# Cross-attention, 16 batches: context of 192 as 128 + 64, loads in order of use, mask on GpSimd

## Chip, core and metric

One core of one Trainium2 chip. The time is that of one execution in microseconds of device time; the median of three runs is given, and one more execution was profiled. Engines: PE (TensorE), DVE (VectorE), ACT (ScalarE), POOL (GpSimd), and SP, whose queue issues most of the DMAs here.

## The reference, cut to what matters

All tensors are float32. B = 16 batches, S = 256 queries of width 256, 77 context rows of width 192, H = 8 heads of D = 256. The mask (16 x 77) is all ones in the inputs.

```python
Q = (img_embed @ Wq).reshape(B, -1, H, D).transpose(0, 2, 1, 3)
K = (sent_embed @ Wk).reshape(B, -1, H, D).transpose(0, 2, 1, 3)
V = (sent_embed @ Wv).reshape(B, -1, H, D).transpose(0, 2, 1, 3)
score = jnp.einsum('bhqd,bhkd->bhqk', Q, K) / math.sqrt(D)
score = jnp.where(mask, score, -jnp.inf)
attn = jax.nn.softmax(score, axis=-1)
ctx = jnp.einsum('bhqk,bhkd->bqhd', attn, V).reshape(B, -1, H * D)
out = ctx @ Wo + img_embed
mu = jnp.mean(out, axis=-1, keepdims=True)
var = jnp.var(out, axis=-1, keepdims=True)
return (out - mu) * jax.lax.rsqrt(var + EPS) * gamma + beta
```

## The kernel before

The weights are folded per head, so that neither Q, K nor V is ever formed. In the setup, `gT` holds Wk Wq^T of each head (tile `pg`, L156) and `u` holds Wv Wo (tile `pu`, L191). For both, slices of the weights are transposed on PE (`transposed`, L135) and copied out of PSUM by `evacuate` (L103), which alternates between ACT and DVE. The context is transposed to `cT` (tile `pc`, L170), and GpSimd copies it into `cM` (the first 64 rows of each batch) and `cR` (the other 13).

The width 192 of the context lies on 96 partitions twice, so every product over it is two matmuls of 96 rows that add up in one PSUM bank. There are three such products: `pr` (L206, rows 64 to 76 of the values, for all batches), `pa` (L264, keys times `gT`: for a group of four batches, 16 outputs of 308 columns), and `pv` (L282, values for a pair of batches, four outputs of 512 columns).

The results of `pr` go through `stage` and a DRAM tensor `scratch` to `vr`, in another layout: eight DMAs per `stage` and one back, all issued by SP. `stage` lies in the memory of the setup pool `wload`; when that pool closes, the pool of `a` takes the memory over, so that the first copies into `a` wait until the DMAs have read `stage`.

The main loop runs over 32 tiles of 128 queries, 8 per group of four batches. `prepare_group` transposes x (tile `px`, copied to `xT`) and makes `a`; `prepare_pair`, every fourth tile, makes `vw` from `pv` with sixteen copies, eight on ACT and eight on DVE. `scores_and_softmax` computes the scores (tile `ps`, two banks; 4 matmuls) and on DVE adds the mask's bias (`s`, L312, which frees `ps`), takes the maximum and subtracts it; ACT takes the exponential (`e`), DVE the sum (`den`, `rden`), GpSimd the product `p`. `attend`, two tiles later, transposes `p` (`pp`, `pq`), copies it to `pT` on ACT, and multiplies with `vw` and `vr` (`po`); DVE adds x. `normalise_group` does the layer norm's last step for eight tiles at once and sends four DMAs.

Each engine runs its instructions in a fixed order. A scheduler that knows the tiles and their buffers sets that order at build time, so an instruction can stand at another place than in the code. PSUM has eight banks: two score buffers of two banks, two for transposes (`ps_tr`), two for products (`ps_mm`).

The mask's arithmetic is on DVE: `bias` is 0 or -3e38, `live` is 1 for a batch with a key left and not a number for one without.

Of the kernel before, what the change touches and what calls it, by code (L numbers as in the profile page):

```python
# [21 lines left out]
MASKED = 3.0e38  # L22

# [10 lines left out]
def kernel(  # L34
# [16 lines left out]
    LP = DL // 2  # L51
    CR = 112
# [10 lines left out]
    assert NCR * CR == B * S2 and NG * GB == B and DI == 2 * P and D == 2 * P  # L63
# [25 lines left out]
    xg_of = {}  # L89
# [6 lines left out]
    dram = ctx.enter_context(tc.tile_pool(name="dram", bufs=1, space=bass.MemoryType.DRAM))  # L96
    scratch = dram.tile([B, H, KR, DI], F32, tag="scratch", name="scratch")

    cM = const.tile([LP, 2, B, KM], F32, tag="cM", name="cM")
    cR = const.tile([LP, 2, B, KR], F32, tag="cR", name="cR")  # L100
    evacs = [0]

    def evacuate(dst, src):  # L103
        evacs[0] += 1
        if evacs[0] % 2:
            nc.scalar.copy(dst, src)  # L106
        else:
            nc.vector.tensor_copy(dst, src)  # L108


    with tc.tile_pool(name="wload", bufs=1) as wp, tc.tile_pool(name="wt", bufs=2) as wt:
# [21 lines left out]
        load_x(1)  # L133
# [16 lines left out]
        for h in range(H):  # L150
# [3 lines left out]
            for lc in range(2):  # L154
                for dc in range(2):
                    nc.tensor.matmul(  # L156
                        pg[:LP, lc, :],
                        wkT[:, dc, lc * LP : (lc + 1) * LP],
# [4 lines left out]
            nc.scalar.mul(gT[:, :, h, :], pg[:LP], D ** -0.5)  # L163

        for r in range(0, NCR, 2):
            n = min(2, NCR - r)
            pc = ps_tr.tile([P, 4, P], F32, tag="tr", name=f"pc_{r}")
            for lc in range(2):
                for j in range(n):
                    nc.tensor.transpose(  # L170
                        pc[:LP, 2 * lc + j, :CR],
                        c_sb[:, r + j, lc * LP : (lc + 1) * LP],
                        ident[:CR, :CR],
                    )
# [208 lines left out]
    for t in range(NT + AHEAD):  # L383
# [44 lines left out]
```

## Time and profile before

| | us |
|---|---|
| median of 3 runs (lowest, highest) | 415.19 (415.14, 417.15) |
| the profiled execution | 414.41 |
| its span (first to last instruction) | 412.4 |
| PE busy | 352.2 (85% of the span) |
| DVE busy | 228.2 (55%) |
| ACT busy | 115.0 (28%) |
| POOL busy | 50.3 (12%) |

The share is a mean over stages. The setup ends at 124 us with the first `ps`; then four groups of about 74 us follow, each opened by its `px` and `pa` (those of the first group stand in the setup). In a row of the timeline, the number in brackets is the time that the engine stood idle just before, with what ended it. A matmul of float32 shows as two records; the duration of a record is its whole way through the array, and the next one starts before it ends, so the distance between starts is what a record costs in a stream.

### The profile page before, as it was taken

Reading aid. Unit: us, or ns where it says so; the run is one execution under the profiler, and the core shown is the slowest. Engines: PE = TensorE matmul, PEld = TensorE weight load, DVE = VectorE, ACT = ScalarE, POOL = GpSimd, SP = SyncE. Lnnn points to the kernel's source line nnn. Section 1 sums busy time; section 2 is a strip of 40 time slices with the busy share of each in tenths; the row PEclk is TensorE's granted clock in tenths of the full one; section 3 lists DMA queues with packets and bytes.
Section 4 is the critical chain, followed back from the end, with each engine's and each line's share of the span. In section 5 each row is a group of like instructions: output and inputs, shape, how many; then the busy total and the mean of one; then the engine's idle time right before and its main releaser. Section 6 shows DMA issues by size and latency. Waiting matters only on the chain.

```text
span 412.4 us, 4082 instructions
## 1 busy us (share of the span) xinstructions
PE 352.2 (85%) x1462; PEld 245.6 (60%) x1462; DVE 228.2 (55%) x492; ACT 115.0 (28%) x246; POOL 50.3 (12%) x74
## 2 busy tenths in 40 slices
PE   0604989994799999999999999999999999999972
PEld 0503767633474657767576676758757775775851
DVE  0004132222025996942699886258988725798884
ACT  1200342111123242231443322243333223334231
POOL 0000002000001121310111221011121201032120
PEclk9955999998599999999999999999999999999997
DMA  8999000026500000000006000000500000030002
GB/s 219 262 287 325 3 0 0 2 63 150 119 2 0 0 0 2 0 2 0 0 2 203 0 2 2 0 0 2 175 28 2 0 2 0 0 103 2 0 1 102
DMA packets 17005, 21.22 MB, mean 51 GB/s; under 512 B 714, under 2 KB 15770, under 8 KB 16794
## 3 DMA queue, kind: packets, MB, share of 16 engines
q1 hardware_dynamic: 13258, 16.36, 14.1%
q10 hardware_dynamic: 3728, 4.62, 4.0%
q8 instruction: 11, 0.18, 0.2%
q14 instruction: 8, 0.07, 0.0%
HBM read 15.08 MB, written 5.90 MB: 51 GB/s over the span
## 4 chain that ended last, share of the span: by engine, by line
PE 47%; DVE 32%; DMA 9%; ACT 7%; issue 3%; SPq 1%; ACTq 0%; DVEq 0%
PE pa L264 16%; PE pv L282 9%; DMA m_i<-in_mask_BxS_if_dram 5%; DVE s L320 5%; DVE top L319 4%; DVE s L312 4%; PE po L354 4%; ACT e L324 4%; PE pg L156 4%; DVE xg L370 4%; PE pu L191 4%; PE ps L304 3%; DVE den L326 3%; PE pr L206 3%; DVE xg L373 3%
## 5 line engine op out<-in xcount | busy, mean ns | idle before, releaser
L333 POOL TENSOR_TENSOR p<-e,rden 128x512 f32<-128x512 f32 x64 | 47.0, 755 | 289.6 <-DVE rden L329 156.3
L264 PE MATMUL pa<-cT,gT 96*128 96x308 f32 x256 | 71.8, 438 | 8.6 <-ACT a L106 8.6
L304 PE MATMUL ps<-a,xT 128*128 128x308 f32 x256 | 75.4, 422 | 0.0
L264 PEld LDWEIGHTS pa<-cT,gT 96*128 96x128 f32 x256 | 49.6, 198 | 26.5 <-ACT a L106 9.0
L354 PE MATMUL po<-vw,pT 128*128 128x256 f32 x256 | 61.1, 381 | 4.7 <-ACT pT L348 4.7
L282 PE MATMUL pv<-u,cM 96*128 96x512 f32 x128 | 60.0, 602 | 3.9 <-ACT vw L292 2.7
L354 PEld LDWEIGHTS po<-vw,pT 128*128 128x128 f32 x256 | 48.1, 190 | 17.2 <-ACT pT L348 7.6
L304 PEld LDWEIGHTS ps<-a,xT 128*128 128x128 f32 x256 | 46.5, 190 | 13.4 <-issue 1.4
L108 DVE COPY a<-pa 128x308 f32<-128x308 f32 x32 | 15.3, 479 | 58.3 <-PE pa L264 49.3
L282 PEld LDWEIGHTS pv<-u,cM 96*128 96x128 f32 x128 | 23.0, 189 | 31.4 <-issue 19.8
L324 ACT ACTIVATE e<-s 128x616 f32<-128x616 f32 x32 | 22.9, 716 | 55.6 <-DVE s L320 55.6
L292 DVE COPY vw<-pv 64x256 f32<-64x256 f32 x64 | 26.9, 421 | 15.1 <-PE pv L282 14.1
L156 PE MATMUL pg<-wqT,wkT 128*96 128x256 f32 x64 | 19.0, 449 | 19.0 <-DVE wkT L108 19.0
L348 ACT COPY pT<-pp 128x512 f32<-128x512 f32 x32 | 18.6, 583 | 56.4 <-PE pp L347 56.2
L326 DVE TENSOR_REDUCE den<-e 128x8 f32<-128x616 f32 x32 | 25.3, 791 | 14.8 <-ACT e L324 14.6
L292 ACT COPY vw<-pv 64x256 f32<-64x256 f32 x64 | 23.4, 365 | 29.4 <-PE pv L282 28.5
L106 ACT COPY a<-pa 128x308 f32<-128x308 f32 x32 | 13.3, 417 | 60.4 <-PE pa L264 50.9
L312 DVE TENSOR_TENSOR s<-ps,bias 128x616 f32<-128x616 f32 x32 | 25.0, 782 | 6.4 <-PE ps L304 6.4
L156 PEld LDWEIGHTS pg<-wqT,wkT 128*96 128x96 f32 x64 | 11.6, 192 | 24.3 <-DVE wkT L108 20.6
L320 DVE TENSOR_TENSOR s<-s,top 128x616 f32<-128x616 f32 x32 | 25.7, 803 | 0.7
L319 DVE TENSOR_REDUCE top<-s 128x8 f32<-128x616 f32 x32 | 25.1, 783 | 0.3
L347 PEld LDWEIGHTS pp<-ident,p 128*128 128x128 f32 x128 | 16.0, 141 | 10.5 <-issue 5.3
(57 smaller groups left out, 305.6 us busy)
## 6 DMA issues: line engine op xcount, KB each, us to landing
xg<-in_x_dram SPq DMA_DIRECT2D x4, 1024.0 KB
out_dram<-xg SPq DMA_DIRECT2D x16, 256.0 KB
wq_sb<-in_L_xattn_Wq_dram SPq DMA_DIRECT2D x2, 1024.0 KB
wo_sb<-in_L_xattn_Wo_dram ACTq DMA_DIRECT2D x1, 2048.0 KB
scratch<-stage SPq DMA_DIRECT2D x16, 104.0 KB
vr<-scratch SPq DMA_DIRECT2D x2, 832.0 KB
wk_sb<-in_L_xattn_Wk_dram ACTq DMA_DIRECT2D x2, 768.0 KB
wv_sb<-in_L_xattn_Wv_dram SPq DMA_DIRECT2D x1, 1536.0 KB
```

The source lines that it names most:

```text
L156: nc.tensor.matmul(pg[:LP, lc, :], wkT[:, dc, lc * LP : (lc + 1) * LP], wqT[:, dc, :], start=(dc == 0), stop=(dc == 1),)
L264: nc.tensor.matmul(pa.rearrange("p b k -> p (b k)"), gT[:, lc, h, dc * P : (dc + 1) * P], cT[:, lc, g * GB * S2 : (g + 1) * GB * S2], star ...
L282: nc.tensor.matmul(pv.rearrange("p h d -> p (h d)"), cM[:, lc, b : b + 2, :].rearrange("p b k -> p (b k)"), u[:, lc, 2 * n : 2 * n + 2, :] ...
L292: copy(vw[i][half * KM : (half + 1) * KM, n, :], pv[i * KM : (i + 1) * KM, half, :],)
L304: nc.tensor.matmul(ps[:, hh, :HK], xT_of[g][:, dc, j * P : (j + 1) * P], a_of[g][:, dc, bl, hh * 4 : hh * 4 + 4, :].rearrange("p h k -> p ...
L312: nc.vector.tensor_tensor(s.rearrange("p (a h) k -> p a h k", a=2), ps[:, :, :HK].rearrange("p a (h k) -> p a h k", k=S2), bias[:, b, :].u ...
L319: nc.vector.tensor_reduce(top, s, AX.X, ALU.max)
L320: nc.vector.tensor_tensor(s, s, top.unsqueeze(2).to_broadcast([P, H, S2]), ALU.subtract)
L324: nc.scalar.activation(e, s, AF.Exp)
L326: nc.vector.tensor_reduce(den, e, AX.X, ALU.add)
L333: nc.gpsimd.tensor_tensor(part, e[:, :, keys], rden.unsqueeze(2).to_broadcast(list(part.shape)), ALU.mult,)
L354: nc.tensor.matmul(po, pT[:, n, :], vw_of[b][:, n, :], start=(n == 0), stop=False)
```

## The change

- The context is split as 128 + 64. The first part (`cA`, `gA`, `uA`) fills all rows of PE. The second (`cB`, `gB`, `uB`) has 64 rows; `cB` is held twice, on partitions 0 to 63 and 64 to 127, and `gB` and `uB` hold even parts in the lower half and odd ones in the upper.
- A helper `products` issues four matmuls of 128 rows, then four of 64 rows that alternate between the halves, each into its own bank; all copies follow after the eight. It is used for `pr`, `pa` and `pv` (not shown: it reads as `pr` with `cMA` and `cMB`, and its 16 copies follow product by product). In the built program the 64-row matmuls carry a tile size of 64 x 128 and a tile position of row 0 or 64; all others have 128 x 128.
- `ps_mm` has four banks, `ps_sc` one score buffer instead of two.
- Loads: context first (half by ACT, half by SP), then x of group 0, then `wq` and `wk` in slices of two heads, `wv` and `wo` in halves, then x of group 1, the mask, gamma and beta, nearly all by SP.
- The context and x of group 0 are transposed before the weights. `pg` and `pu` are copied out by two instructions each (the 128-row and the 64-row part); of `pg`, ACT copies the first and DVE the second.
- The mask's arithmetic is on GpSimd, as products over halves of the keys.
- The last group is normalised in two parts: six tiles after tile 29, the other two at the end.

```diff
-    ps_sc = ctx.enter_context(tc.tile_pool(name="ps_sc", bufs=2, space=PSUM))
+    ps_sc = ctx.enter_context(tc.tile_pool(name="ps_sc", bufs=1, space=PSUM))
...
-    ps_mm = ctx.enter_context(tc.tile_pool(name="ps_mm", bufs=2, space=PSUM))
+    ps_mm = ctx.enter_context(tc.tile_pool(name="ps_mm", bufs=4, space=PSUM))
...
+    gA = const.tile([P, H, DI], F32, tag="gA", name="gA")
+    gB = const.tile([P, NF, DI], F32, tag="gB", name="gB")
+    uA = const.tile([P, H, DI], F32, tag="uA", name="uA")
+    uB = const.tile([P, NF // 2, 2, DI], F32, tag="uB", name="uB")
...
+    def half(i):
+        return slice(i * LB, (i + 1) * LB)
...
+    def products(outs, weightA, weightB, movingA, movingB):
+        for i in range(4):
+            nc.tensor.matmul(outs[i], weightA(i), movingA(i), start=True, stop=False)
+        for i in range(4):
+            nc.tensor.matmul(outs[i], weightB(i), movingB(i), start=False, stop=True)
...
-        half = H * D // 2
-        for i in range(2):
-            cols = slice(i * half, (i + 1) * half)
+        wo_r = wo.rearrange("(t p) f -> p t f", p=P)
+        mid = NCR // 2
+        nc.scalar.dma_start(c_sb[:, :mid, :], c_rows[:, :mid, :])
+        nc.sync.dma_start(c_sb[:, mid:, :], c_rows[:, mid:, :])
+        load_x(0)
+        for h in range(0, H, 2):
+            cols = slice(h * D, (h + 2) * D)
             nc.sync.dma_start(wq_sb[:, :, cols], wq_r[:, :, cols])
-            nc.scalar.dma_start(wk_sb[:, :, cols], wk_r[:, :, cols])
-        nc.scalar.dma_start(c_sb, c_rows)
-        nc.sync.dma_start(wv_sb, wv_r)
-        nc.scalar.dma_start(wo_sb, wo.rearrange("(t p) f -> p t f", p=P))
-        load_x(0)
+            nc.sync.dma_start(wk_sb[:, :, cols], wk_r[:, :, cols])
+        for h in range(0, H, 4):
+            cols = slice(h * D, (h + 4) * D)
+            nc.sync.dma_start(wv_sb[:, :, cols], wv_r[:, :, cols])
+            nc.sync.dma_start(wo_sb[:, 2 * h : 2 * h + 8, :], wo_r[:, 2 * h : 2 * h + 8, :])
+        load_x(1)
         nc.sync.dma_start(m_i, mask.rearrange("b k -> (b k)").partition_broadcast(P))
         nc.sync.dma_start(gam, gamma.partition_broadcast(P))
         nc.sync.dma_start(bet, beta.partition_broadcast(P))
-        load_x(1)
...
+            rows = slice(r * CR, (r + n) * CR)
+            evacuate(flat(cA)[:, rows].rearrange("p (j m) -> p j m", m=CR), pc[:, :n, :CR])
+            for i in range(2):
+                evacuate(
+                    flat(cB)[half(i), rows].rearrange("p (j m) -> p j m", m=CR),
+                    pc[LB:, 2 : 2 + n, :CR],
+                )
...
+        transpose_x(0)
...
+            nc.scalar.mul(gA[:, h, :], pg[:, 0, :], D ** -0.5)
+            nc.vector.tensor_scalar(
+                gB[half(h % 2), h // 2, :], pg[LB:, 1, :], D ** -0.5, None, ALU.mult
+            )
...
-            evacuate(u[:, :, h, :], pu[:LP])
+            evacuate(uA[:, h, :], pu[:, 0, :])
+            n = h // 2
+            evacuate(uB[half(n % 2), n // 2, h % 2, :], pu[LB:, 1, :])
+        nc.gpsimd.tensor_scalar(bias_f, m_i, 0.0, None, ALU.is_equal)
+        none = wp.tile([P, B, S2 // 2], F32, tag="none", name="none")
+        left, n = bias, S2
+        while n > 1:
+            n, odd = n // 2, n % 2
+            nc.gpsimd.tensor_tensor(none[:, :, :n], left[:, :, :n], left[:, :, n : 2 * n], ALU.mult)
+            if odd:
+                nc.gpsimd.tensor_tensor(
+                    none[:, :, :1], none[:, :, :1], left[:, :, 2 * n : 2 * n + 1], ALU.mult
+                )
+            left = none
+        none = none[:, :, 0]
+        nc.gpsimd.tensor_scalar(none, none, MASKED, MASKED, ALU.mult, ALU.mult)
+        nc.gpsimd.tensor_tensor(live, none, none, ALU.subtract)
+        nc.gpsimd.tensor_scalar(live, live, 1.0, None, ALU.add)
+        nc.gpsimd.tensor_scalar(bias_f, bias_f, -MASKED, None, ALU.mult)
...
+            products(
+                pr,
+                lambda n: flat(cRA[:, batches, :]),
+                lambda n: flat(cRB[half(n % 2), batches, :]),
+                lambda n: flat(uA[:, 2 * n : 2 * n + 2, :]),
+                lambda n: flat(uB[half(n % 2), n // 2, :, :]),
+            )
+            for n in range(NF):
+                evacuate(flat(stage[:, 2 * n : 2 * n + 2, :]), pr[n])
...
+            pa = [
+                ps_mm.tile([P, GB, S2], F32, tag="mm", name=f"pa_{g}_{n}_{i}") for i in range(4)
+            ]
+            products(
+                [flat(o) for o in pa],
+                lambda i: gA[:, 2 * n + i % 2, i // 2 * P : (i // 2 + 1) * P],
+                lambda i: gB[half(i % 2), n, i // 2 * P : (i // 2 + 1) * P],
+                lambda i: flat(cA[:, batches, :]),
+                lambda i: flat(cB[half(i % 2), batches, :]),
+            )
+            for i in range(4):
+                evacuate(a[:, i // 2, :, 2 * n + i % 2, :], pa[i])
...
-            if d % GT == GT - 1:
-                normalise_group(d // GT)
-                if d // GT + 2 < NG:
-                    load_x(d // GT + 2)
+            if d // GT == NG - 1:
+                if d % GT == GT - QT - 1:
+                    normalise(d // GT, 0, GT - QT)
+                elif d % GT == GT - 1:
+                    normalise(d // GT, GT - QT, GT)
+            elif d % GT == GT - 1:
+                normalise(d // GT, 0, GT)
+            if d % GT == GT - 1 and d // GT + 2 < NG:
+                load_x(d // GT + 2)
```

On DVE near the start of the program, before: `wkT` is the transposed key weight of a head, `m_i` the mask as loaded, `some` and `live` results of the mask.

```order
L108 COPY wkT_0_123<-p_wkT_0_124 128x384
L230 TENSOR_SCALAR bias_80<-m_i_101 128x1232
L232 TENSOR_REDUCE some_477<-bias_80 128x16
L233 RECIPROCAL live_81<-some_477 128x16
L235 TENSOR_SCALAR bias_80<-bias_80 128x1232
L108 COPY wkT_1_143<-p_wkT_1_144 128x384
L234 TENSOR_TENSOR live_81<-live_81,some_477 128x16
```

And after, the same place, behind the copies of the context and x:

```order
L127 COPY xT_0_178<-px_0_6_197 128x2x256
L127 COPY wkT_0_210<-p_wkT_0_211 128x384
L235 TENSOR_SCALAR gB_80<-pg_0_217 64x256
L127 COPY wkT_1_231<-p_wkT_1_232 128x384
L235 TENSOR_SCALAR gB_80<-pg_1_238 64x256
L127 COPY wkT_2_252<-p_wkT_2_253 128x384
```

The mask has left DVE's queue; between two `wkT` copies there stands now the copy of the 64-row part of `pg` of the head before.

On PE after the first `ps` of a group (tile 16, the third group), before: the products `pv` of a pair are mixed with the work of the tiles 14, 15 and 17.

```order
L282 MATMUL pv_8_2_1548<-u_78,cM_88 128x512 x2
L347 MATMUL pp_14_1563<-ident_70,p_14_1358 128x128 x2
L350 MATMUL pq_14_1569<-ident_70,p_14_1358 104x128
L304 MATMUL ps_17_1582<-a_2_1446,xT_2_1421 128x308
L282 MATMUL pv_8_3_1555<-u_78,cM_88 128x512 x2
L354 MATMUL po_14_1572<-vw_7_1252,pT_14_1562 128x256 x4
L355 MATMUL po_14_1572<-vr_82,pT_14_1562 128x256
L304 MATMUL ps_17_1582<-a_2_1446,xT_2_1421 128x308 x3
L347 MATMUL pp_15_1603<-ident_70,p_15_1398 128x128 x4
L350 MATMUL pq_15_1609<-ident_70,p_15_1398 104x128
L304 MATMUL ps_18_1648<-a_2_1446,xT_2_1421 128x308 x2
L354 MATMUL po_15_1612<-vw_7_1252,pT_15_1602 128x256 x4
```

After:

```order
L151 MATMUL pv_8_3_1580<-uB_82,cMB_86 128x512
L396 MATMUL pp_14_1606<-ident_72,p_14_1401 128x128 x4
L399 MATMUL pq_14_1612<-ident_72,p_14_1401 104x128
L353 MATMUL ps_17_1625<-a_2_1489,xT_2_1464 128x308 x2
L403 MATMUL po_14_1615<-vw_7_1295,pT_14_1605 128x256 x4
L404 MATMUL po_14_1615<-vr_89,pT_14_1605 128x256
L353 MATMUL ps_17_1625<-a_2_1489,xT_2_1464 128x308 x2
L396 MATMUL pp_15_1646<-ident_72,p_15_1441 128x128 x4
L399 MATMUL pq_15_1652<-ident_72,p_15_1441 104x128
L353 MATMUL ps_18_1691<-a_2_1489,xT_2_1464 128x308
L403 MATMUL po_15_1655<-vw_7_1295,pT_15_1645 128x256 x4
```

The eight matmuls of `pv` now stand in one piece ahead of the transposes `pp_14`; `po` stands between pieces of `ps`, as it did.

## Rows read from the trace of the kernel before

**Rows 1.** Page part 2: PE's busy tenths in 40 slices of 10.3 us

```profile
PE   0604989994799999999999999999999999999972
```

**Rows 2.** Windows: stretch, each engine's busy us (count), granted PE clock, DMA share, GB/s

```profile
0.00:20.00 20.00, 6.82 (x28) 5.24 (x28) 0.62 (x2) 3.63 (x5) 0.70 (x6) 1.00 0.94 241
20.00:40.00 20.00, 3.72 (x10) 2.52 (x11) 3.69 (x6) 0.00 (x0) 0.00 (x0) 0.52 1.06 312
...
106.00:112.00 6.00, 5.89 (x12) 3.91 (x13) 0.68 (x2) 0.47 (x2) 0.00 (x0) 0.50 0.69 145
```

**Rows 3.** Timeline 0 to 50 us: start, us, engine, line, operation [idle before, releaser]

```profile
32.55 0.80 DVE L230 TENSOR_SCALAR bias<-m_i 128x1232 f32<-128x1232 int32 x1 [19.34 <-DMA m_i<-in_mask_BxS_if_dram]
...
36.28 3.73 PE L156 MATMUL pg<-wqT,wkT 128*96 128x256 f32 x8 [17.91 <-DVE wkT L108]
...
44.25 1.97 PE L156 MATMUL pg<-wqT,wkT 128*96 128x256 f32 x8 [0.21 <-DVE wkT L108]
...
47.20 1.97 PE L156 MATMUL pg<-wqT,wkT 128*96 128x256 f32 x8 [0.21 <-DVE wkT L108]
```

**Rows 4.** Timeline 62 to 128 us, setup's second half

```profile
62.30 3.69 PE L191 MATMUL pu<-wo_sb,wvT 128*96 128x256 f32 x16
...
79.78 13.90 PE L206 MATMUL pr<-u,cR 96*104 96x512 f32 x32
...
87.62 7.15 SPq L218 DMA_DIRECT2D scratch<-stage  x9
...
105.63 0.42 ACT L106 COPY a<-pa 128x308 f32<-128x308 f32 x1 [9.49 <-DMA scratch<-stage]
...
124.04 2.24 PE L304 MATMUL ps<-a,xT 128*128 128x308 f32 x8
```

**Rows 5.** Groups by form: line, engine, tiles, shapes, count, busy, mean ns, idle before

```profile
L304 PE MATMUL ps<-a,xT 128*128 128x308 f32 x256 | 75.4, 422 | 0.0
...
L292 DVE COPY vw<-pv 64x256 f32<-64x256 f32 x64 | 26.9, 421 | 15.1 <-PE pv L282 14.1
...
L292 ACT COPY vw<-pv 64x256 f32<-64x256 f32 x64 | 23.4, 365 | 29.4 <-PE pv L282 28.5
...
L206 PE MATMUL pr<-u,cR 96*104 96x512 f32 x32 | 13.9, 592 | 0.0
...
L333 POOL TENSOR_TENSOR p<-e,rden 128x104 f32<-128x104 f32 x32 | 14.4, 451 | 0.0
...
L108 DVE COPY cT<-pc 96x224 f32<-96x224 f32 x5 | 1.8, 385 | 3.3 <-ACT cT L106 3.3
```

**Rows 6.** Timeline 251 to 342 us, one group of eight tiles

```profile
251.69 15.71 PE L264 MATMUL pa<-cT,gT 96*128 96x308 f32 x60
...
267.25 2.24 PE L304 MATMUL ps<-a,xT 128*128 128x308 f32 x8
...
277.81 1.89 PE L354 MATMUL po<-vw,pT 128*128 128x256 f32 x8
...
286.76 0.77 DVE L312 TENSOR_TENSOR s<-ps,bias 128x616 f32<-128x616 f32 x1
286.86 2.24 PE L304 MATMUL ps<-a,xT 128*128 128x308 f32 x8
...
314.18 0.77 DVE L312 TENSOR_TENSOR s<-ps,bias 128x616 f32<-128x616 f32 x1
...
319.78 0.77 DVE L312 TENSOR_TENSOR s<-ps,bias 128x616 f32<-128x616 f32 x1
...
324.46 0.66 DVE L108 COPY xT<-px 128x512 f32<-128x512 f32 x1
...
341.22 2.24 PE L304 MATMUL ps<-a,xT 128*128 128x308 f32 x8
```

**Rows 7.** Timeline 385 to 413 us, DVE at the end

```profile
404.36 0.43 DVE L357 TENSOR_TENSOR xg<-po,xg 128x256 f32<-128x256 f32 x1 [2.14 <-PE po L355]
...
406.13 3.26 DVE L373 SCALAR_TENSOR_TENSOR xg<-xg,rstd,bet 128x256 f32<-128x256 f32 x8
```

More of the change, by code (lines that the diff above doesn't have):

```diff
@@ L156 @@
                     nc.tensor.matmul(
[L157 to L158 removed]
+                        pg[:, lc, :],
+                        wkT[:, dc, lc * LB : lc * LB + P],
                         wqT[:, dc, :],
@@ L201 @@
+        none = none[:, :, 0]
[3 more added lines that the diff above has]
+        nc.gpsimd.tensor_scalar(bias_f, bias_f, -MASKED, None, ALU.mult)
         for r in range(B // RB):
             stage = wp.tile([RB * KR, H, DI], F32, tag=("c", "wq")[r], name=f"stage_{r}")
[L203 to L216 removed]
+            pr = [
+                ps_mm.tile([P, 2 * DI], F32, tag="mm", name=f"pr_{r}_{n}")[: RB * KR]
+                for n in range(NF)
+            ]
+            batches = slice(r * RB, (r + 1) * RB)
+            products(
[4 more added lines that the diff above has]
+                lambda n: flat(uB[half(n % 2), n // 2, :, :]),
+            )
+            for n in range(NF):
+                evacuate(flat(stage[:, 2 * n : 2 * n + 2, :]), pr[n])
@@ L278, in prepare_pair @@
         vw = [ap.tile([P, NF, DI], F32, tag="vw", name=f"vw_{b + i}", bufs=4) for i in range(2)]
-        for n in range(NF):
-            pv = ps_mm.tile([P, 2, DI], F32, tag="mm", name=f"pv_{b}_{n}")
-            for lc in range(2):
-                nc.tensor.matmul(
-                    pv.rearrange("p h d -> p (h d)"),
-                    cM[:, lc, b : b + 2, :].rearrange("p b k -> p (b k)"),
-                    u[:, lc, 2 * n : 2 * n + 2, :].rearrange("p h d -> p (h d)"),
-                    start=(lc == 0),
-                    stop=(lc == 1),
-                )
+        pv = [ps_mm.tile([P, 2, DI], F32, tag="mm", name=f"pv_{b}_{n}") for n in range(NF)]
+        products(
+            [flat(o) for o in pv],
+            lambda n: flat(cMA[:, b : b + 2, :]),
+            lambda n: flat(cMB[half(n % 2), b : b + 2, :]),
+            lambda n: flat(uA[:, 2 * n : 2 * n + 2, :]),
+            lambda n: flat(uB[half(n % 2), n // 2, :, :]),
+        )
+        for n in range(NF):
             copy = nc.vector.tensor_copy if n % 2 else nc.scalar.copy
             for i in range(2):
-                for half in range(2):
-                    copy(
-                        vw[i][half * KM : (half + 1) * KM, n, :],
-                        pv[i * KM : (i + 1) * KM, half, :],
-                    )
+                for j in range(2):
+                    copy(vw[i][half(j), n, :], pv[n][half(i), j, :])
         vw_of[b], vw_of[b + 1] = vw
@@ L360, in attend, with normalise @@
         nc.vector.bn_aggr(mv_of[g][:, j, :], bn)
-    def normalise_group(g):
+    def normalise(g, first, last):
         mv, yg = mv_of[g], xg_of[g]
-        std = st.tile([P, GT], F32, tag="std", name=f"std_{g}", bufs=2)
-        nc.scalar.activation(std, mv[:, :, 1], AF.Sqrt, bias=eps)
-        rstd = st.tile([P, GT], F32, tag="rstd", name=f"rstd_{g}", bufs=2)
-        nc.vector.reciprocal(rstd, std)
-        for j in range(GT):
+        std = st.tile([P, GT], F32, tag="std", name=f"std_{g}_{first}", bufs=2)
+        nc.scalar.activation(std[:, first:last], mv[:, first:last, 1], AF.Sqrt, bias=eps)
+        rstd = st.tile([P, GT], F32, tag="rstd", name=f"rstd_{g}_{first}", bufs=2)
+        nc.vector.reciprocal(rstd[:, first:last], std[:, first:last])
+        for j in range(first, last):
             y = yg[:, j, :]
```

137 lines of the change are left out of this document (54 added, 83 removed).

## Prediction

> **What bounds the kernel now.** I read the page's tenths first: TensorE (PE) stands at 9 nearly everywhere from slice 10 on, with one hole in slices 2 and 3 and one in slice 9 (a slice is 10.3 us) [rows 1]. So there are two questions: what the holes are, and what the stretch is worth where PE is full. The timeline answers the first. The mask arithmetic of VectorE (DVE) waits until 32.55 for the mask's load; the wkT copy of the next head stands behind it in DVE's queue, so PE idles 17.9 us before pg at 36.28 [rows 3]. The second hole is the first copy of `a`, which reuses the memory of `stage` and waits until 105.63 for the last DMA into `scratch`; SP issues these DMAs one after another from 87.62 on [rows 4]. For the second question I read the groups by form and the timeline of one group of eight tiles (251 to 342 us). A context of 192 is contracted as 96 + 96, and each such matmul is issued as two records (32 of pr for 16 in the code). A record of 308 columns takes 0.259 us of the stream (60 in 15.71), one of 512 columns 0.43 us (32 in 13.9) [rows 5, 6]. In the tile stretch DVE is nearly as full as PE: from one `s` to the next it needs 5.6 us (314.18 to 319.78) [rows 6]. That matters below: there PE time saved is not time saved.
>
> **The mask and the loads (pg to pu).** With the mask on GpSimd, the 17.9 us wait and the half-speed records after it go (eight pg records take 3.73 us at 36.28 and 1.97 at 44.25; the granted clock of 20 to 40 us is 0.52, mostly the 1.2 GHz level, with PE idle ahead) [rows 2, 3]. What is late next? The new order loads c (0.95 MB) and x (1.05 MB) ahead of wq and wk; at 241 GB/s [rows 2] and, as an estimate, 2 us before data flows, c is there at about 6 us, x at 10, the first two heads at 13. Before pg can start, PE must transpose c and x: six tiles of c with three copies each out of one bank, which take turns on ScalarE (ACT) and DVE, 6 to 7.5 us by the present 0.39 us per copy [rows 5] and PE at its slow pace; four tiles of x, 2.5 to 4.4; two heads of weights, 2 to 3. So pg starts at 16.5 to 21.5, and I take 18.5. A head takes 2.95 us now (44.25 to 47.20) [rows 3]; the order shows the new copy gB, which waits for ACT's gA, ahead of the next wkT on DVE: about 2.0 us until ACT starts, 0.38 + 0.42 for the two copies (nearest rows: 64x256 copies, 365 and 421 ns [rows 5]), 0.56 for wkT, so 3.45 us. Eight heads end at 44.7. The pu stretch took 17.5 us (62.30 to 79.78) [rows 4] and has one more copy per head, partly in PE's way: 18.9. So pr starts at 63.6, not 79.78: **-16.2 us**. GpSimd's own mask work costs nothing: by 241 and 312 GB/s [rows 2] the mask lands at about 42 us; its 14 operations, small ones at 0.45 us [rows 5] and even at 2 us each, end by 75, and `s` needs the result after 100. Without that cover they would cost 10 to 30 us.
>
> **Row halves, pr and the first pa.** The 128-row records stay at today's pace. The 64-row ones are four per product set, lower and upper half alternating, two records each. No row of the trace shows two matmuls side by side. The bounds: no overlap (8 slots for 8 records) and full overlap (4). Both records of one matmul use the same rows, and records on the same rows follow each other here; so I take 5 slots: only the second record of one meets the first of the next. For pr: 3.44 + 2.15 us per set, last copy at 6.6 us after the start, where SP now begins after 7.84 (79.78 to 87.62). From SP's first issue to the copy of `a` is 18.0 us [rows 4] and stays (same DMAs, same queue), so `a` starts at 24.6 and PE 0.5 later. Four of the 16 outputs of pa are then done; three sets of 2.07 + 1.30 us are left, 10.1 us, plus 3.0 because the clock comes back late, as now: after 8 us of idle the granted clock is 0.50 (1.2 GHz) from 106 to 112 us, and 12 records take 5.89 us, twice their later pace [rows 2]. That is 38.2 us from pr to the first ps, against 44.3 (79.78 to 124.04) [rows 4]: **-6.1 us**.
>
> **Tile stretch of a group.** Times count from the group's first ps (267.25 before) [rows 6]. The four products of pv now end at 7.7 us, but their copies come all at the end: ACT needs 1.5 us for each of two products (four of 0.365), so it is free for pT at 9.6 and po starts at 10.3, before at 10.6 (277.81). About 2 us of PE time thus give 0.3. Then comes the single score buffer: ps of a tile must wait until DVE has read the one before. Today ps starts at 286.86, while `s` of the tile before runs from 286.76 to 287.53 [rows 6]; going on with DVE's 5.6 us per tile, PE waits 0.6 to 0.8 us at four tiles of a group. Queued behind are pp and po of earlier tiles, and for them DVE's add. By this chain DVE reaches the xT copy of the next group at 58.1 us, before at 57.2 (324.46): **+0.9 us** per group. Then pa: 16.8 us before (324.46 to 341.22) [rows 6], now 1.5 + 14 x 0.518 + 4 x 1.30 = 13.9: -2.9. Three groups with both: **-6.0**; the last stretch, with no pa behind it: **+0.9**.
>
> **Tail.** Eight final operations of 0.41 us stand at the end (406.13, 3.26 us); six of them move ahead of the last tile's, where DVE idles 2.1 us, and push its add back by 0.4 [rows 7]: **-2.0 us**.
>
> **Change of tile shape.** 26 sets go from 128 to 64 rows and back. Bounds: nothing, or per change what one record takes beyond its stream, 0.42 - 0.26 = 0.16 us [rows 5, 6]. I take the middle, on the 18 sets of pa and pr (pv's hide behind ACT's copies): 36 x 0.09 = **+3.2 us**.
> The Trainium skill (TensorEngine Tiling (Array Packing), section Key Properties) says that switching the tiling mode drains TensorE; no row here shows a switch, and by the full 0.16 us the sum would be 2.6 us longer. The same page of the Trainium skill (section Theoretical Speedup) gives up to 2x for a dimension of at most 64; by that the 4-slot bound would hold, which is the third rival.
>
> **Sum.** -16.2 - 6.1 - 6.0 + 0.9 - 2.0 + 3.2 = -26.2. The profiled execution took 414.41 us for a span of 412.4; so a span of 386.2 and a time of 388.2. The median of the runs stands 0.8 above the profiled one: **389 us**.
>
> **Rivals.**
> - No overlap: the records of both halves simply follow each other. For it: nothing in the trace overlaps. Each pa set is 0.78 us longer, and pv's copies start later: 3.6 us in each of three groups, 3.6 in pr and the first pa, 0.5 at the end: +15, **404 us**.
> - Score buffer dearer than worked out: po stands between the first and the last piece of ps in the new order, so each tile is a chain PE, DVE, PE. Half a microsecond more at 24 tiles is +12: **401 us**. Against it: 0.52 + 2.16 + 1.56 us of PE work plus 0.8 of `s` stays under DVE's 5.6.
> - Full halves and free switches: -3.1 in pa of three groups, -1.2 before, -3.2: **381 us**; with an early start of pg 378.
> - Slower than before: 64-row records that don't stream but take their whole recorded time, 422 and 592 ns [rows 5]. The pa sets get 2.1 us longer (16 times), pr 2.6 (twice), pv's add about 15 after the copies' cover, less the 3 for switches: +50, **439 us**. It decides from about 0.9 us per set over my value; today's pace without overlap is 0.8 in pa. Against it: every 96- and 104-row record streams now.
> - The change doesn't do what it says: if the mask, though on GpSimd, still held DVE, 18 us would stay, 407 us. Nothing in DVE's new order up to the first `s` reads the mask; this is in the last 0.02.
>
> **How the numbers follow.** Forecast 0.40, no overlap 0.22, full halves 0.19, score buffer 0.12, slower 0.05, the rest 0.02. The likeliest is 389. The low end takes full halves with pg at 16.5 or earlier (376), the high end no overlap with dear switches (406). Faster by over 0.5% (about what a measurement of this kernel can tell from no change) 0.93, same 0.02, slower 0.05.
>
> **What the new profile would show.** Step one: no PE idle over 2 us between the first pg and pr, pr near 64 us, a pg period of 3.4. Step two: 64-row pa records 0.16 us apart on average mean 5 slots, 0.13 full overlap, 0.26 none; PE still waits for `scratch` about 10 us, with a granted clock of 0.5 behind it. Step three: PE waits for DVE's `s` at ps, two to four times a group, and 72 us from the first ps of one group to the next. The forecast is wrong if pg starts after 22, if 64-row records take over 0.26 us, or if a group still takes 74.

## The result and the profile after

The changed kernel takes **385.89 us** (median of 4 runs, 385.51 to 386.57), the kernel before on the same chip 415.16 (413.78 to 417.15): a ratio of 0.9293, 95% interval 0.9253 to 0.9334. The forecast was 389 within 376 to 406. The profiled execution took 386.57 for a span of 384.8, so the span shrank by 27.6 us (from 412.4) where the sum said 26.2.

The page's tenths and granted clock by slice (9.6 us now), beside [rows 1]:

```profile
PE   1887898935999988998998999988988998998982
...
PEclk9999999995999999999999999999999999999998
```

Slices are counted from 0. The first hole is gone: slices 1 to 3 show 8, 8 and 7, where 6, 0 and 4 stood. The second is still there, in slices 8 and 9. From slice 10 on PE is a little less full than before: eleven slices show 8, where nearly all showed 9.

The windows of the places that [rows 2] showed before (stretch, busy us of PE, PEld, DVE, ACT, POOL, then the granted clock, DMA share, GB/s):

```profile
20.00:40.00 20.00, 16.23 (x92) 13.35 (x92) 5.48 (x11) 5.44 (x11) 0.00 (x0) 1.00 1.04 298
...
80.00:91.00 11.00, 0.57 (x6) 0.08 (x2) 0.22 (x1) 0.41 (x2) 0.00 (x0) 0.74 0.60 146
91.00:97.00 6.00, 5.94 (x17) 3.46 (x18) 1.28 (x4) 0.94 (x4) 0.00 (x0) 0.63 0.64 145
```

From 20 to 40 us PE now works 16.2 us at a granted clock of 1.00 (2.4 GHz), where it worked 3.7 at 0.52. After the idle time before 91 the clock is low again (0.63 in the mean from 91 to 97).

The setup in the timeline (start, us, engine, line, operation, [idle before, releaser]), beside [rows 3, 4]:

```profile
7.09 1.73 PE L187 MATMUL pc<-ident,c_sb 112*128 112x112 f32 x8 [7.09 <-DMA c_sb<-in_ctx_dram]
...
20.79 1.99 PE L227 MATMUL pg<-wqT,wkT 128*128 128x256 f32 x8
...
40.92 3.34 POOL L257 TENSOR_SCALAR bias<-m_i 128x1232 f32<-128x1232 int32 x1 [23.66 <-DMA m_i<-in_mask_BxS_if_dram]
...
66.06 3.60 PE L149 MATMUL pr<-uA,cRA 128*104 128x512 f32 x8
...
72.40 5.79 SPq L292 DMA_DIRECT2D scratch<-stage  x9
...
90.58 0.74 ACT L125 COPY a<-pa 128x308 f32<-128x308 f32 x2 [12.90 <-DMA vr<-scratch]
...
91.06 4.47 PE L149 MATMUL pa<-cA,gA 128*128 128x308 f32 x8 [10.48 <-ACT a L125]
...
103.82 2.34 PE L353 MATMUL ps<-a,xT 128*128 128x308 f32 x8
```

It is POOL that now waits 23.7 us for the mask's load, and nobody waits for POOL there. The first pg comes at 20.79 (36.28 before), pr at 66.06 (79.78), the first ps at 103.82 (124.04).

The last `pa` of the trace and the tile stretch behind an earlier one:

```profile
252.74 1.99 PE L403 MATMUL po<-vw,pT 128*128 128x256 f32 x8 [1.12 <-ACT pT L397]
...
298.56 1.04 PE L136 MATMUL px<-ident,xg 128*128 128x128 f32 x8
...
304.04 2.34 PE L149 MATMUL pa<-cA,gA 128*128 128x308 f32 x8
306.31 1.31 PE L151 MATMUL pa<-cB,gB 64*128 64x308 f32 x8
307.60 2.34 PE L149 MATMUL pa<-cA,gA 128*128 128x308 f32 x8
...
314.67 1.56 PE L353 MATMUL ps<-a,xT 128*128 128x308 f32 x5
```

What PE waited for (total us, times, longest; before, it was 4.7 us for pT and none for `s`):

```profile
PE po L403 <- ACT pT L397: 14.0, 17, 1.1
PE pa L149 <- ACT a L125: 10.5, 1, 10.5
...
PE ps L353 <- DVE s L361: 5.6, 15, 0.8
```

The same list for one group alone, from its first ps to the next px: before (267.25 to 321.85 us), then changed (242.19 to 298.56 us):

```profile
PE pv L282 <- ACT vw L292: 0.9, 2, 0.6
PE po L354 <- ACT pT L348: 0.6, 1, 0.6
```

```profile
PE po L403 <- ACT pT L397: 3.5, 4, 1.1
PE ps L353 <- DVE s L361: 1.4, 4, 0.3
```

Three numbers from such timelines sort out all kernels below: the first ps, the **tile stretch** (from a group's first ps to the first transpose px of the next group) and the **pa part** (from that px to the next first ps). The table gives them for the third group; the stretch of the first group is shorter (50.2 us before, 49.8 changed), and in the last group the tail stands behind it. The px of the kernel before, the last row also being the end of the stretch that begins at 267.25 [rows 6]:

```profile
247.87 1.04 PE L251 MATMUL px<-ident,xg 128*128 128x128 f32 x8
...
321.85 1.04 PE L251 MATMUL px<-ident,xg 128*128 128x128 f32 x8
```

| kernel | us | ratio to before (95%) | first ps | tile stretch | pa part |
|---|---|---|---|---|---|
| before | 415.16 | | 124.0 | 54.6 | 19.4 |
| changed | 385.89 | 0.929 (0.925 to 0.933) | 103.8 | 56.4 | 16.1 |
| one_half | 406.65 | 0.983 (0.980 to 0.985) | 108.4 | 57.0 | 20.1 |
| by_pairs | 390.13 | 0.942 (0.940 to 0.945) | 104.9 | 55.8 | 17.5 |
| turn_about | 382.31 | 0.924 (0.921 to 0.927) | 103.3 | 55.7 | 16.0 |
| before_mask | 394.11 | 0.954 (0.950 to 0.957) | 104.5 | 54.6 | 19.4 |
| mask_dve | 385.41 | 0.932 (0.930 to 0.934) | 102.7 | 56.4 | 16.1 |
| one_score | 426.71 | 1.032 (1.027 to 1.036) | 123.1 | 58.7 | 18.4 |
| two_scores | 387.03 | 0.935 (0.932 to 0.938) | 104.0 | 54.9 | 16.6 |
| split_pair | 393.56 | 0.952 (0.948 to 0.955) | 103.3 | 58.3 | 16.1 |
| one_normalise | 388.39 | 0.938 (0.935 to 0.940) | 103.5 | 56.4 | 16.1 |
| far_stage | 385.51 | 0.931 (0.929 to 0.934) | 102.7 | 56.4 | 16.1 |
| open_stage | 373.76 | 0.904 (0.901 to 0.907) | 90.9 | 56.4 | 16.1 |
| open_turn | 370.30 | 0.895 (0.892 to 0.898) | 90.0 | 55.7 | 16.0 |

(The kernel before had medians of 413.1 to 415.2 beside these; the ratios go by the runs of the same chip. far_stage, which changes nothing in the order, stands 0.4 us off the changed kernel, so smaller differences between rows say nothing.)

### The profile page after: what moved, and what is told of

It reads as the page before. It is cut to its first block, busy times and chain, and to the rows that moved or that the text cites. A ratio compares the mean times of both kernels' runs of the same rounds, so it can differ in the third digit from the quotient of the medians.

```text
span 384.8 us, 4113 instructions
## 1 busy us (share of the span) xinstructions
PE 331.6 (86%) x1462; PEld 226.2 (59%) x1462; DVE 228.9 (59%) x503; ACT 118.3 (31%) x254; POOL 62.6 (16%) x88
## 4 chain that ended last, share of the span: by engine, by line
PE 63%; DVE 17%; ACT 10%; DMA 4%; issue 2%; SPq 2%; POOL 0%; ACTq 0%; DVEq 0%; POOLq 0%
PE po L403 11%; PE ps L353 10%; PE pa L149 9%; PE pv L149 7%; ACT vw L344 5%; PE pa L151 5%; PE pg L227 4%; PE pu L244 4%; DVE s L361 3%; PE pv L151 3%; PE po L404 3%; ACT pT L397 2%; DMA scratch<-stage 2%; PE px L136 2%; SPq L292 2%
## 5 line engine op out<-in xcount | busy, mean ns | idle before, releaser
L382 POOL TENSOR_TENSOR p<-e,rden 128x512 f32<-128x512 f32 x64 | 47.8, 767 | 273.6 <-DVE rden L378 164.7
L353 PE MATMUL ps<-a,xT 128*128 128x308 f32 x256 | 77.1, 430 | 5.6 <-DVE s L361 5.6
L403 PE MATMUL po<-vw,pT 128*128 128x256 f32 x256 | 62.2, 386 | 14.0 <-ACT pT L397 14.0
L403 PEld LDWEIGHTS po<-vw,pT 128*128 128x128 f32 x256 | 47.2, 190 | 26.9 <-ACT pT L397 19.9
L149 PE MATMUL pa<-cA,gA 128*128 128x308 f32 x128 | 40.3, 452 | 10.5 <-ACT a L125 10.5
L149 PEld LDWEIGHTS pa<-cA,gA 128*128 128x128 f32 x128 | 23.6, 198 | 23.4 <-ACT a L125 16.2
L397 ACT COPY pT<-pp 128x512 f32<-128x512 f32 x32 | 18.8, 586 | 51.7 <-PE pp L396 51.3
L149 PE MATMUL pv<-uA,cMA 128*128 128x512 f32 x64 | 28.8, 592 | 0.0
L406 DVE TENSOR_TENSOR xg<-po,xg 128x256 f32<-128x256 f32 x32 | 13.4, 418 | 18.8 <-PE po L404 18.8
L151 PE MATMUL pa<-cB,gB 64*128 64x308 f32 x128 | 20.9, 445 | 0.0
L419 DVE SCALAR_TENSOR_TENSOR xg<-xg,mv,gam 128x256 f32<-128x256 f32 x32 | 19.8, 620 | 0.1
## 6 DMA issues: line engine op xcount, KB each, us to landing
scratch<-stage SPq DMA_DIRECT2D x16, 104.0 KB
```

What stands on the lines that cost most here:

```text
L149: nc.tensor.matmul(outs[i], weightA(i), movingA(i), start=True, stop=False)
L151: nc.tensor.matmul(outs[i], weightB(i), movingB(i), start=False, stop=True)
L353: nc.tensor.matmul(ps[:, hh, :HK], xT_of[g][:, dc, j * P : (j + 1) * P], flat(a_of[g][:, dc, bl, hh * 4 : hh * 4 + 4, :]), start=(dc == 0) ...
L382: nc.gpsimd.tensor_tensor(part, e[:, :, keys], rden.unsqueeze(2).to_broadcast(list(part.shape)), ALU.mult,)
L397: nc.scalar.copy(pT[:, :NF, :], pt)
L403: nc.tensor.matmul(po, pT[:, n, :], vw_of[b][:, n, :], start=(n == 0), stop=False)
```

## The experiments

**Do the row halves overlap?** one_half puts all 64-row operands into rows 0 to 63, for instance

```diff
-gB[half(h % 2), h // 2, :], pg[LB:, 1, :]
+gB[:, h, :], pg[LB:, 1, :]
```

> The changed kernel with all 64-row operands in rows 0 to 63, so that no two neighbouring products stand in different row halves; everything else is the same, also the order on every engine. Theory (the halves overlap fully, the eight 64-row records of a pa set take 4 slots of 0.26 us): the part then takes 8 slots, 2.07 us in place of 1.04; the wait for the copy of pa shrinks, since outputs finish one by one, so a set goes from 3.56 to 4.35 to 4.6 us, 16 sets +13 to +17; pr +1.7 per set; pv +1.7 per pair, half of it under ACT's copies: 386 + 13..17 + 3.4 + 0..14, 402 to 420 us. The prediction's sizing (5 slots): 8 slots are 0.78 us more per pa set, 401 us. Rival (nothing overlaps, the time came from elsewhere): 386, and 64-row records 0.26 us apart in both kernels.

It took 406.65 us, 20.8 more. PE's timeline of one_half:

```profile
166.31 2.34 PE L149 MATMUL pa<-cA,gA 128*128 128x308 f32 x8
168.58 2.34 PE L151 MATMUL pa<-cB,gB 64*128 64x308 f32 x8
170.85 2.34 PE L149 MATMUL pa<-cA,gA 128*128 128x308 f32 x8
```

Eight 64-row records last as long as eight 128-row ones, 2.27 us from start to start; in the changed kernel they take 1.29 (306.31 to 307.60). So the halves do overlap, and the overlap is worth 0.98 us per set of pa. A narrow cut of the changed kernel's timeline (306.30 to 306.33 us) holds two of these records, which start together and are both done after 0.53 us:

```profile
306.31 0.53 PE L151 MATMUL pa<-cB,gB 64*128 64x308 f32 x2
```

**What does a change of tile shape cost?** by_pairs changes four times per set, turn_about once (the edits in short; A is a 128-row matmul, B a 64-row one):

```diff
-for i in range(4): A(i)
-for i in range(4): B(i)
+for j in (0, 2): A(j), A(j + 1), B(j), B(j + 1)
```

```diff
+turn[0] = 1 - turn[0]
 parts = [(weightA, movingA), (weightB, movingB)]
+if turn[0]: parts.reverse()
```

> The changed kernel with each set of products in the order A0 A1 B0 B1 A2 A3 B2 B3 (A: 128 rows, B: 64 rows), so four changes of tile shape per set in place of two, while the copy of the first outputs can start half a set earlier. A pa set takes 3.56 us now, of which 3.11 is the stream (8 x 0.26 + 4 x 0.26). Theory (half of the 0.45 us left over is the wait for a free bank, the change of shape itself costs 0.1): 3.3 to 3.5 us a set and no wait of PE for the copy of pa, 382 to 386 us. Rival (the change of shape takes all of it, 0.22 us each): 4.0 us a set, 26 sets of 0.45 us, part of pv covered: 393 to 398 us. By the prediction's 0.09 us per change: 3.29 without the bank wait to 3.5 with it, 384 to 388.

> The changed kernel with every second set of products begun with its 64-row part (A B, B A, A B ...), so half as many changes of tile shape, and the same number of records. Theory (a change costs 0.1 to 0.2 us, the rest of the gap is the wait for a bank): the 64-row part that follows another needs its banks at twice the pace, so the wait for a bank stays or grows; 26 changes fewer give at most 2.6 to 5, half of it eaten: 383 to 387 us. Rival (a change costs 0.22 us and nothing else is in the gap): 26 x 0.22 = 5.7 less, 380 us.

PE's timeline of by_pairs:

```profile
158.30 1.30 PE L150 MATMUL pa<-cA,gA 128*128 128x308 f32 x4
159.54 0.79 PE L152 MATMUL pa<-cB,gB 64*128 64x308 f32 x4
160.26 1.30 PE L150 MATMUL pa<-cA,gA 128*128 128x308 f32 x4
161.49 0.79 PE L152 MATMUL pa<-cB,gB 64*128 64x308 f32 x4
```

and of turn_about:

```profile
155.95 2.70 PE L155 MATMUL pa<-cB,gB 64*128 64x308 f32 x16
158.58 4.41 PE L155 MATMUL pa<-cA,gA 128*128 128x308 f32 x16
162.93 2.70 PE L155 MATMUL pa<-cB,gB 64*128 64x308 f32 x16
```

Sixteen 128-row records and a change take 4.35 us (158.58 to 162.93), eight and a change 2.27 (one_half), four and a change 1.24 (158.30 to 159.54). Eight records more cost 2.08, so one takes 0.26 and the change 0.19. The way back, from 64 rows to 128, costs the same in one_half, where eight 64-row records and a change also take 2.27. In by_pairs four 64-row records and a change take 0.72: two slots of 0.26 and 0.20. So **a change costs 0.2 us in either direction, and the overlap is full**: 8 records in 4 slots. A set of the changed kernel, 3.56 us, is 12 slots (3.10), two changes (0.40) and 0.05 left over, which I put down to waiting for a bank. My expectation of 0.1 us per change was wrong, and the rival's 0.22 nearly right. Both times, 390.13 and 382.31 us, lie between what theory and rival gave. by_pairs got slower by 4.2 us: 16 sets of pa at 0.35 more are 5.6, and some came back, since its wait for pT is 9.4 us and not 14.0.

turn_about gained 3.6, but its pa part only 0.14 per group: where two 64-row parts follow each other, 16 records take 2.63, with 0.36 beyond 8 slots and a change. Most of the gain is in the tile stretch (0.64 per group, 1.4 in the first group), and PE's wait for pT fell from 14.0 to 11.1 us. A set of pv that ends with its 128-row part hands over its outputs one by one and not all at the end. In turn_about the two sets of a group end differently, the first with its 64-row part and the second with its 128-row part, and the waits behind them differ too:

```profile
249.86 1.99 PE L407 MATMUL po<-vw,pT 128*128 128x256 f32 x8 [1.11 <-ACT pT L401]
...
277.47 1.99 PE L407 MATMUL po<-vw,pT 128*128 128x256 f32 x8 [0.55 <-ACT pT L401]
```

In the changed kernel, where both sets end with the 64-row part, both waits are 1.12 us. So the wait goes with the order of the parts; no run changes the order of pv alone.

**The first hole: which part of the change closed it?** before_mask is the kernel before with nothing but the mask arithmetic of the changed kernel, on GpSimd; mask_dve is the changed kernel with the same arithmetic on VectorE (the first line of that edit):

```diff
-nc.gpsimd.tensor_scalar(bias_f, m_i, 0.0, None, ALU.is_equal)
+nc.vector.tensor_scalar(bias_f, m_i, 0.0, None, ALU.is_equal)
...
```

> The kernel before with nothing but the mask arithmetic of the changed kernel on GpSimd in place of that on VectorE; loads, products and buffers stay. Theory (the wait for the mask in DVE's queue held PE for 17.9 us and made the records behind it slow for 1.8 more): pg runs from 18.4 on, pr starts near 60, first ps near 104: 394 to 396. By the prediction's split, in which loads in a new order are part of the 16.2 us: 397 to 400. Rival (the stall goes to the next late thing, the second halves of wq and wk or c): 403 to 410.

> The changed kernel with the 14 mask operations on VectorE in place of GpSimd; loads and all other work stay. VectorE's order then has five of them between the wkT copy of the seventh head and the gB copy of that head, near 42 us, when the mask (landed at 40.9 in the changed kernel) is there. Theory (what cost 18 us in the kernel before was the place in the queue ahead of a late load, not the engine): no wait for the load, only the operations themselves, some 4 us by 0.79 us for 616 columns plus ten small ones of 0.2, partly beside PE's work: 388 to 392. Rival (the engine is what matters, the queue stalls as before): PE idles over 10 us, 400 to 405. Other rival (all of it lies beside other work): 386.

before_mask took 394.11, 19.4 us less than the kernel before on its chip (413.55). So this one edit makes some two thirds of the whole gain, and all the others together add about 8 us. Its pr starts at 59.63, 20.2 us earlier than in the kernel before and 6.4 earlier than in the changed one. In mask_dve no wait for the load is left either (DVE, PE in its timeline):

```profile
41.45 0.79 DVE L257 TENSOR_SCALAR bias<-m_i 128x1232 f32<-128x1232 int32 x1
...
45.62 1.99 PE L227 MATMUL pg<-wqT,wkT 128*128 128x256 f32 x8 [0.25 <-DVE wkT L127]
```

DVE reaches the first mask operation at 41.45, when the mask is there. The first five of the 14 operations take 3 us out of its queue, and PE waits 0.25. The engine is not what counts: where the operation stands in DVE's queue, relative to the landing of its load, is. The cost of 2 to 6 us that I expected did not come: the operations of 1232 columns took 0.79 us each, half of what I had worked out, and DVE has room in this stretch.

**The single score buffer.** one_score makes that edit alone in the kernel before; two_scores undoes it in the changed kernel, with the transposes' banks taken from the products.

```diff
-ps_sc = ctx.enter_context(tc.tile_pool(name="ps_sc", bufs=2, space=PSUM))
+ps_sc = ctx.enter_context(tc.tile_pool(name="ps_sc", bufs=1, space=PSUM))
```

```diff
-ps_sc = ctx.enter_context(tc.tile_pool(name="ps_sc", bufs=1, space=PSUM))
-ps_tr = ctx.enter_context(tc.tile_pool(name="ps_tr", bufs=2, space=PSUM))
+ps_sc = ctx.enter_context(tc.tile_pool(name="ps_sc", bufs=2, space=PSUM))
-ps_tr.tile(..., tag="tr")
+ps_mm.tile(..., tag="mm")
```

> The kernel before with one score buffer in place of two, the edit of the changed kernel alone (ps_mm stays at two banks). Theory (the prediction's, PE waits 0.6 to 0.8 us for s at four tiles of a group but DVE sets the pace): PE waits 5 to 12 us for s, the time grows by 1 to 4 us, 415 to 418. Rival (each tile a chain PE, DVE, PE, half a microsecond at 24 tiles or more): 424 to 430. Other rival (no cost): 413.6.

> The changed kernel with two score buffers again; the two banks come from the pool of the transposes, whose tiles share the four banks of the products. Theory (with one buffer each tile is a chain PE, DVE, PE, which cost 4.1 us per group in the kernel before and costs near 2 here, and eats what pv gains): the stretch from a group's first ps to the next px goes from 56.4 to 54 or less and PE's wait for s goes; if the transposes do not miss their banks, 376 to 380. Rival (they miss them: pp and px wait for copies of pv and po, as many us as the score buffer gives): 384 to 392, and this run then says nothing on the buffer's price.

one_score is 13.2 us slower, at the price of the rival. Its timeline shows the chain at its longest:

```profile
294.97 1.30 PE L304 MATMUL ps<-a,xT 128*128 128x308 f32 x4 [1.39 <-DVE s L312]
```

PE's waits for `s` come to 10.3 us in all, but the tile stretch grows by 4.1 in each full group (3.5 in the first): what stands behind ps comes late too. The price includes the order that the scheduler builds for one buffer, in which ps is cut into other pieces than before. two_scores (387.03) does not price the buffer in the changed order. PE's wait for `s` is gone, but new waits are there:

```profile
PE pp L395 <- POOL p L381: 8.7, 6, 2.4
...
PE po L402 <- ACT pT L396: 6.0, 10, 1.9
```

Its tile stretches are 47.4, 56.8 and 54.9 us in the first three groups, against 49.8, 56.4 and 56.4 in the changed kernel. This one stays inconclusive.

**What PE waits for in the tile stretch.** split_pair makes the four products of pv as two and two, one loop turn apart.

```diff
-if t % (2 * QT) == 0:
-    prepare_pair(t // QT)
+if t % (2 * QT) < 2:
+    prepare_pair(t // (2 * QT) * 2, t % (2 * QT))
```

> The changed kernel with the four products of pv made in two pairs, one loop turn apart (A0 A1 B0 B1, then A2 A3 B2 B3 with the next tile), so that ACT copies two pieces of vw of 1.5 us and not one of 3.0 ahead of a pT copy. Theory (in the tile stretch PE now waits mostly for pT, 14 us in all, behind ACT's vw copies): that wait falls to 5 or less, two more changes of tile shape per pair cost 8 x 0.4 = 3.2: 378 to 383. Rival (DVE's 5.6 us per tile set the pace and PE's wait only moves to s): 385 to 389.

It took 393.56, more than theory and rival gave, and the wait for pT grew:

```profile
PE po L407 <- ACT pT L401: 21.1, 24, 1.1
```

The theory falls. The timeline shows why a shorter burst does not help:

```profile
251.25 1.49 ACT L349 COPY vw<-pv 64x256 f32<-64x256 f32 x4
...
252.75 0.59 ACT L401 COPY pT<-pp 128x512 f32<-128x512 f32 x1
...
253.39 1.99 PE L407 MATMUL po<-vw,pT 128*128 128x256 f32 x8 [0.85 <-ACT pT L401]
```

After every visit of pv the pT copy stands behind vw copies that can't begin before pv's end, and the wait is about 1 us whether four copies stand there or eight (0.85 to 1.09 here, 1.12 in the changed kernel). Two visits per pair make two such waits: six waits for pT in a group, where the changed kernel has four.

**The tail.** one_normalise normalises the last group in one go again.

```diff
-if d % GT == GT - QT - 1:
-    normalise(d // GT, 0, GT - QT)
-elif d % GT == GT - 1:
-    normalise(d // GT, GT - QT, GT)
+if d % GT == GT - 1:
+    normalise(d // GT, 0, GT)
```

> The changed kernel with the last group normalised in one go after its last tile, as before. By the prediction's term: 2.0 us longer, 387.5 to 388.5. Theory from the trace of the changed kernel (six final operations of 0.41 us, 2.44 us, stand at 375.63 in a time in which VectorE would else wait for po, and delay the last add a little): +1.5 to +2.5. Rival (the out transfers, which also start earlier for six tiles, are the last thing): +3 or more.

388.39, 2.5 us more (the last stretch alone grows by 2.3). At the end of one_normalise and then of the changed kernel:

```profile
379.85 3.25 DVE L422 SCALAR_TENSOR_TENSOR xg<-xg,rstd,bet 128x256 f32<-128x256 f32 x8
```

```profile
375.63 2.44 DVE L422 SCALAR_TENSOR_TENSOR xg<-xg,rstd,bet 128x256 f32<-128x256 f32 x6
...
380.33 0.88 DVE L422 SCALAR_TENSOR_TENSOR xg<-xg,rstd,bet 128x256 f32<-128x256 f32 x2
```

**The second hole.** far_stage only creates the load tiles in another order, so that `a` lies where wk and wv were and shares no byte with stage (this follows from the order in which the tiles are created; no trace shows addresses). open_stage takes stage from pools that don't close at the end of the setup:

```diff
-wq_sb, wk_sb, wv_sb, wo_sb, c_sb, m_i
+wk_sb, wv_sb, wo_sb, m_i, c_sb, wq_sb
```

```diff
-stage = wp.tile([RB * KR, H, DI], F32, tag=("c", "wq")[r], name=f"stage_{r}")
+stage = (const.tile(..., tag="stage") if r else xp.tile(..., tag="xT"))
```

> The changed kernel with the load tiles created in another order (wk, wv, wo, mask, c, wq), so that the memory of `a` falls on wk and wv and not on the memory that stage takes over; the order on every engine is the same. Theory (the wait of 10.5 us of PE before the second set of pa and the half-speed records behind it come from this reuse of memory alone): PE goes on from pr to pa, the granted clock stays at 1.00, the first ps comes 13.5 us earlier, near 90: 372 us. Rival 1 (the copies wait for SP's queue in any case): 386. Rival 2 (the next reader of that queue is late, po waits for vr, or e and s fall on stage's memory): 376 to 384.

> The changed kernel with stage taken from pools that stay open (stage_0 in the second buffer of xT, stage_1 beside the constants; to make room wvT shares wkT's buffers and the mask's scratch tile c's), so that the first copy of `a` waits for the loads and the mask work alone and not for the DMAs into scratch. Theory (far_stage changed nothing although `a` then lay on other memory, so the wait belongs to the pool that closes, not to the bytes): PE goes on after the first set of pa, no 10.5 us of idle, granted clock 1.00, first ps near 90 in place of 103.8; 371 to 374 us. Rival (the queue of DMAs is the limit anyway, or po waits for vr): 380 to 386.

far_stage changed nothing, and the wait is the same one:

```profile
89.79 0.74 ACT L125 COPY a<-pa 128x308 f32<-128x308 f32 x2 [12.92 <-DMA vr<-scratch]
...
90.26 4.16 PE L149 MATMUL pa<-cA,gA 128*128 128x308 f32 x8 [10.50 <-ACT a L125]
```

In open_stage it is gone, though SP issues the same DMAs at the same time (timeline, then a window):

```profile
72.08 5.79 SPq L295 DMA_DIRECT2D scratch<-stage  x9
...
79.80 0.90 ACT L125 COPY a<-pa 128x308 f32<-128x308 f32 x2 [2.45 <-PE pa L151]
...
80.28 2.34 PE L149 MATMUL pa<-cA,gA 128*128 128x308 f32 x8
```

```profile
80.00:91.00 11.00, 10.97 (x51) 6.47 (x49) 3.18 (x7) 2.74 (x7) 0.00 (x0) 1.00 0.61 153
```

So, as far as these two runs show, the first tile of the new pools waits for whatever still reads a tile of the pool that has closed, whether they share memory or not. The section on the kernel before puts this wait down to shared memory; the wait stays without it. PE's idle 10.5 us and the low clock behind it (1.00 now) are both gone: 12.1 us.

**Together.** open_turn joins open_stage and turn_about.

> open_stage and turn_about together: the stage tiles in pools that stay open, and every second set of products begun with its 64-row part. If the two are independent (one before the first ps, one at every set): 373.8 - 3.6 = 370 us. Rival (turn_about's gain came from the setup alone, as an order of sets that suits the hole): 373 to 374.

370.30 us: the two add up, and this version beats both kernels.

## Why the prediction was right, point by point

- **The mask and the loads** (-16.2, measured -13.7, pr at 66.06 and not 63.6). The mechanism held: the 17.9 us wait and the half-speed records went. The step that failed is the start of pg, taken as 18.5 and measured as 20.79, inside its bounds of 16.5 to 21.5: PE began on c at 7.09 (6 forecast) and had the last x transposed at 18.2. From there the transposes of c took 7.5 us, the upper bound of 6 to 7.5. The pg period was 3.52 (3.45 forecast, though the terms named for it add up to 3.36), the stretch from pu to pr 18.8 (18.9). But the step credited the change's parts together, and before_mask shows their split: the mask alone brings pr 20.2 us forward, the rest of the new setup (order of loads, x transposed earlier, copies in two parts) takes 6.4 back, and pr and pa then return 7.1 (44.9 us in before_mask, 37.8 here). GpSimd itself was not needed (mask_dve).
- **pr and the first pa** (-6.1, measured -6.5: 44.3 to 37.8). The chain held: SP began 6.3 us after pr's start (6.6 forecast), `a` at 24.5 (24.6). The reason given for the hole, that `a` reuses the memory of stage [rows 4], was not the one that counts: in far_stage the wait stays without it, and in open_stage, where stage is in no closing pool, it goes. The number did not hang on it.
- **Slots and changes of shape.** Two sizes were off and cancelled. I took 5 slots, since both records of a matmul use the same rows; it is 4, which is 0.26 x 16 + 0.43 x 2 = 5.0 us less. I took 0.09 us per change; it is 0.20, which is 36 x 0.11 = 4.0 more. That the two nearly cancel is luck. The sign set for 5 slots, 64-row records 0.16 us apart, came true as well (1.29 / 8), but for another reason: 4 slots, a change and 0.05. By that sign alone the two could not be told apart. What the Trainium skill says (TensorEngine Tiling (Array Packing), section Theoretical Speedup), up to 2x for a dimension of at most 64, is borne out here in full: less the change and the 0.05, 2.07 us become 1.03. What the Trainium skill says of a change of tiling mode, that it drains TensorE (the same page, section Key Properties), agrees with the 0.2 us per change here, more than the 0.16 that I had set as the upper bound; no run shows that the time is a drain. The rival "full halves and free switches" had the first half right and the second wrong.
- **The tile stretch** (+0.9 per group, measured +1.8) and **pa** (-2.9 plus four sets' share of the changes, 0.7; measured -3.3). Together -1.5 per group against -1.3, and -3.3 in the first. The step that was too small is this stretch, and its cost does not lie where the text put it. The text put all of it on the single score buffer, with about 11 us of waits for `s` in all; they are 5.6. The larger wait is for pT, behind pv's copies: 3.5 us in the group listed above, 0.6 before. There the text had po gain 0.3 us, but the first po stands 10.55 us behind the first ps (252.74 less 242.19), as before (10.56). The stretch follows the pT wait in other runs: in turn_about the wait of a full group falls to 2.9 and the stretch by 0.64; in by_pairs it falls to 2.2, four more changes of shape cost 0.8, and the stretch falls by 0.52. pv's saving itself is mostly lost behind the copies, as forecast: one_half puts 3.4 us of PE time per group back into pv, and the stretch grows by only 0.66. The score buffer's price in the old order is 4.1 us per full group and 13.2 us in all, about the +12 that the rival put on it; why no more than 1.8 shows here is not settled.
- **The rival without overlap** was put at 404; one_half made it true and took 406.65. The rival of 64-row records that don't stream is excluded by the same rows: eight of them in one half take 2.27 us.
- **The tail** (+0.9 - 2.0): the last stretch went from 71.2 us (341.22 to 412.4) to 70.1 (314.67 to 384.8), -1.1 as forecast, and the split normalise alone is worth 2.5.

The sum came out within 1.4 us with terms off by 2.5, 5.0, 4.0 and 1 to 2 us: a sum that holds does not vouch for its terms.

What stays open: the price of the single score buffer in the new order (at most about 2.4 us per group, an estimate that puts the whole 1.8 and the 0.66 that pv saved on it; the wait for pT has a share that no run separates), which part of the new setup takes the 6.4 us back, and how much of turn_about's gain is the order of outputs in pv.

## What to carry to other kernels

A late load hurts through the queue behind its first reader: move the reader behind work that doesn't need it, on whichever engine, before moving work to another engine. Look at what a pool's end waits for; a tile that a slow DMA still reads belongs into a pool that stays open. Contracting 128 + 64 with the 64-row parts in alternating halves saves a quarter of the slots of 96 + 96, less 0.2 us for each change of shape, so group the parts and let adjacent sets share a shape; and price a double buffer that the critical chain uses (13.2 us here, in the old order) before you give it up for the banks.

## What the runs showed of the hardware

- 64-row records in alternating halves overlap fully even though each matmul is two records: with the change of shape, 8 records of 308 columns take 1.29 us from start to start, 2.27 in one half; without it, 1.03 and 2.07.
- A change between 128-row and 64-row records costs 0.20 us, in both directions, beyond the records' stream.
- GpSimd took 3.34 us for the mask operation of 1232 columns that VectorE does in 0.79 (mask_dve).
- PE's granted clock is 0.63 in the 6 us behind 10.5 us of idle, and 1.00 where the sets of pa follow without that idle time (open_stage, 80 to 91 us).
